# Folding attention's input normalisation into its projection weights, and a new split of the scan input between two engines

## The chip, the core and the metric

The kernel runs on one NeuronCore of one Trainium2 chip. The core has five engines that run their own instruction streams in order and meet at semaphores: PE (TensorE, matrix products), DVE (VectorE, elementwise work and scans), ACT (ScalarE, activations and copies), POOL (GpSimd, elementwise work) and SP (SyncE, which here issues the DMAs). The metric is the time of one execution on the device in microseconds (us); lower is better.

## The reference, cut to what matters

Two layers, each x = x + f(gn(x)), on x of 8 samples x 512 channels x 2304 positions. gn is a group normalisation over 32 groups of 16 channels, without learned scale or shift:

```python
def _gn(v, G=32, eps=1e-5):
    ...
    return ((g - m) / jnp.sqrt(s + eps)).reshape(v.shape)

x = x + _L0_conv_ref(_gn(x), Wq, bq, Wkv, bkv)     # causal linear attention, 8 heads of 64
x = x + _L1_conv_ref(_gn(x), in_proj_w, ...)       # four chained Mamba blocks of 128 channels
```

Attention: q, k, v are W gn(x) + b; Q = elu(q) + 1 and K = elu(k) + 1; the output is the causal sum over positions of (Q_l . K_m) v_m, divided by Q_l . cumsum(K)_l + 1e-10. Mamba: from each block's 128 channels a gate, a short convolution, Silu, and from these the steps delta, B and C; then for 256 channels x 16 states the recurrence h_t = exp(delta_t A) h_(t-1) + delta_t x_t B_t, and y_t = sum over states of h_t C_t. Block s + 1 takes in block s's output.

## The kernel before, in words

**Tiling.** Positions go in six chunks of LC = 384. The Mamba part is 192 *jobs* (8 samples x 4 blocks x 6 chunks); two streams, the even and the odd samples, take turns every six jobs. A job is 8 *slots*; a slot is one half of the 256 channels and 4 of the 16 states, laid out as 128 partitions x 4 groups x 384 positions in a tile u (five buffers). For slot k the program issues

- POOL: `last_product` (L872), the last TAIL = 152 positions of B x (delta x), two slots ahead (L879);
- ACT: `inputs` (L860), a copy of B's first 232 positions for two slots into PSUM (Bp, L863); `decay` (L896), four exponentials of 128x385 into PSUM banks (L900), up to three ahead of the scans (DEPTH);
- DVE: `product` (L887), the first 232 positions (L890), one slot ahead; then four scans (L910);
- POOL: `weigh` (L920), u times C (L923); PE: `gather` (L935), which sums the states by four matmuls into the bank yp (L937), one or two slots later.

`slot` (the loop at the end) writes this order out by hand; every engine runs its list in order. At slot 2 the previous job's sums are gated by DVE (`gated`, L949) and yp is started anew by ACT (`skip`, L868). Slot 7 also issues DVE's product for slot 1 of the next job, behind the one for slot 0 that it issues at its start.

**Tasks beside the slots.** The rest is written as generators that yield due times, counted in half slots; `beside` steps those that are due, twice a slot, so their instructions fall into the engines' lists between scans:

- `statistics` (L225): 24 `bn_stats` on DVE per sample (L253), one every PERIOD = 16 half slots (one job), then `group_norm` (L178), which gives norm[:, 0] = 1/sigma and norm[:, 1] = -mean/sigma per channel (L211). For samples 2 and up it starts so early that two samples' statistics run side by side.
- `chunk` (L280): attention for one sample, 128 output channels o and 384 positions; 192 in all, six to a *part* (sample, o), one per job. In the first part of a sample (o = 0) POOL normalises the input tile xn in four pieces (L324) and it is written to DRAM for the three other parts (L332); PE projects q, k, v (L300, 12 matmuls); ACT takes exp and relu of q and k with the bias (L312, L313); DVE combines them (L359, L367); PE and ACT form the running sum of K (L373, L382), transposes, states and the denominators den (L405); DVE adds 1e-10 and takes the reciprocal (L433, L434); scores, output and state sums follow (L467 to L508). `load_projections` (L99) fetches the next part's weights, two buffers deep, at chunk 4 of 6.
- `prepare` (L710): a job's convolution (L722) and gate matmuls (L733), then on ACT a burst of four Silus (L758 to L763) with an activation table load before and one behind (L900), the steps (L769, L782, L793), delta x on POOL (L834) and the DMAs that spread the rows. The burst falls into slot 7.
- `pass_on` (L578): mixes a block's output into the next block's input and sums the final output on POOL (L696).

The six PSUM banks that decays, projections and all tasks share are handed out in program order (`take`, `Banks`). Before the first job 196 us go into the first statistics and the first chunks of attention; the last dozen jobs have no attention beside them.

Of the kernel before, what the change touches and what calls it, by code (L numbers as in the profile page):

```python
# [9 lines left out]
F32 = mybir.dt.float32  # L10
# [9 lines left out]
LC = 384  # L20
NI, NQ, NGR = 4, 4, 4
SLOTS = 8
TAIL = 152
BANKS = 6
DEPTH = 3
LEAD = 11
# [23 lines left out]
def attention_then_mamba_kernel(  # L50
# [64 lines left out]
    def load_scales():  # L115
# [3 lines left out]
        nc.scalar.activation(w_a, w_a, AF.Exp)  # L119
        nc.scalar.mul(w_a, w_a, -1.0)  # L120

    power = cpool.tile([P, 4], F32, name="power")
    nc.gpsimd.memset(power, -0.5)

# [95 lines left out]

    norms, xns, x1s, done, ksums = {}, {}, {}, {}, {}

    def statistics(b):  # L225

        xv = x[b].rearrange("(t p) l -> p t l", p=P)
        stats = small.tile([P, 4, NC, 6], F32, tag="stats_a", name=f"stats_a{b}", bufs=2)
        if b == 0:

            xs = []

            def load(c):
                t = mpool.tile([P, 4, 1 + LC], F32, tag="u", name=f"xs_{c}", bufs=5)[:, :, 0:LC]
                nc.sync.dma_start(out=t, in_=xv[:, :, c * LC : (c + 1) * LC])
                xs.append(t)

            for c in range(5):
                load(c)
            load_projections()  # L240
            for c in range(NC):
                for ct in range(4):
                    nc.vector.bn_stats(stats[:, ct, c, :], xs[c][:, ct, :])
                if c == 0:
                    load(5)
                    fetch(0)
        else:
            when = begins[b] + b % 2
            for i in range(4 * NC):
                yield (when - 4, 1) if b > 1 else "1", 0  # L250
                xs = piece(b, i)
                yield (when, 1) if b > 1 else "1", 0
                nc.vector.bn_stats(stats[:, i // NC, i % NC, :], xs)  # L253
                when += PERIOD
        norms[b] = yield from group_norm(stats, 4, f"a{b}", 2)

    def piece(b, i):
# [7 lines left out]
    def fetch(m):  # L265

        if m == len(parts):
            return
        b, o, c = parts[m]
        if (o, c) == (0, 0):  # L270
            xns[b] = dpool.tile([512, L], F32, tag="xn", name=f"xn_{b}", bufs=B)
            x1s[b] = dpool.tile([512, L], F32, tag="x1", name=f"x1_{b}", bufs=B)
        xn = apool.tile([P, 4, LC], F32, tag="xn", name=f"xn_{b}_{o}_{c}", bufs=2)
        src = (x[b] if o == 0 else xns[b]).rearrange("(t p) l -> p t l", p=P)
        nc.sync.dma_start(out=xn, in_=src[:, :, c * LC : (c + 1) * LC])
        fetched[m] = xn

    read, passes = [0], {}

    def chunk(m):  # L280

# [9 lines left out]
        def at(j, gap=1):  # L291
            return times[m] + j, gap
# [4 lines left out]
        def project(j):  # L297
            ps = bank()[:, 0:LC]
            for kt in range(4):
                nc.tensor.matmul(  # L300
                    ps,
                    wqs[m // NC][:, kt, j * P : (j + 1) * P],
                    xn[:, kt, :],
                    start=(kt == 0),
                    stop=(kt == 3),
                )
            return ps, bqkv_sb[:, j * 4 + o : j * 4 + o + 1]

        def feature(ps, bias):

# [2 lines left out]
            nc.scalar.activation(ps, ps, AF.Relu, bias=bias)  # L313
            return ex

        if o == 0:
            yield at(-4), 0
            while b not in norms or m not in fetched:
                yield "1w", 0
            xn, norm = fetched.pop(m), norms[b]  # L320
            for ct in range(4):
                if ct:
                    yield at(ct - 4), 0
                nc.gpsimd.tensor_scalar(  # L324
                    xn[:, ct, :],
                    xn[:, ct, :],
                    norm[:, 0, ct : ct + 1],
                    norm[:, 1, ct : ct + 1],
                    ALU.mult,
                    ALU.add,  # L330
                )
# [4 lines left out]
        if o:  # L336
            xn = fetched.pop(m)
# [46 lines left out]
        yield at(7), 0  # L384
        pr = new("pr")
        nc.vector.tensor_mul(pr, q, kc)
        bank.free()
# [2 lines left out]
        for src in (k, vT):  # L390
            ps = bank()[:, 0:LC].rearrange("p (i t) -> p i t", i=NT)
            for i in range(NT):
                nc.tensor.transpose(ps[:, i, :], src[:, subs[i]], ident)
            turned.append(ps)
        yield at(9), 0
        kl, v = new("kl", 1, (P, NT, P)), new("v", 2, (P, NT, P))
        nc.scalar.copy(kl, turned[0])
# [3 lines left out]
        yield at(12), 1  # L401
        both = bank()
        den = both[:, 0 : 2 * NT]
        for i in range(NT):
            nc.tensor.matmul(den[:, 2 * i : 2 * i + 2], pr[:, subs[i]], hsel, start=True, stop=True)  # L405
        more = NT if c + 1 < NC else NT - 1
        ds = both[:, LC - NT * 64 : LC].rearrange("p (i d) -> p i d", i=NT)
        place = range(NT + 1) if c % 2 == 0 else range(NT, -1, -1)
# [113 lines left out]
    class Stream:  # L522
# [55 lines left out]
        def pass_on(self):  # L578
# [78 lines left out]
            for c in range(NC):  # L657
# [13 lines left out]
                if old is None:  # L671
                    nc.scalar.activation(xi[:, icols], xb, AF.Identity, **normed)
                else:
                    bank = Banks()
                    mixed = bank()[:, 0:LC]
                    more = len(factors) == 3
                    for i, src in enumerate((xi[:, icols], fu)):
                        nc.tensor.matmul(  # L678
                            mixed, mix[:, i, :], src, start=i == 0, stop=i == 1, skip_group_check=True
                        )  # L680
                    yield "1", 0
                    nc.scalar.copy(fu, mixed)
# [20 lines left out]
    class Job:  # L703
# [155 lines left out]

        def inputs(self, pair):  # L860

            self.Bp = psx.tile([P, 2, LC - TAIL], F32, tag="Bp", name=f"Bp_{self.n}_{pair}")
            nc.scalar.copy(self.Bp, self.B[pair % 2][:, :, 0 : LC - TAIL])  # L863

        def skip(self, h):

# [4 lines left out]

        def last_product(self, s):  # L872

            shape, cols = [P, NGR, TAIL], slice(LC - TAIL, LC)
            h, q = s // NQ, s % NQ
            u = mpool.tile([P, NGR, 1 + LC], F32, tag="u", name=f"u_{self.n}_{s}", bufs=5)
            if self.c:
                nc.scalar.copy(u[:, :, 0], self.state[:, h, q, :])
            nc.gpsimd.tensor_tensor(  # L879
                u[:, :, 1 + LC - TAIL :],  # L880
                self.B[q // 2][:, q % 2, cols].unsqueeze(1).to_broadcast(shape),
                self.dxr[h][:, :, cols],
                ALU.mult,
# [2 lines left out]

        def product(self, s, u):  # L887

            shape, cols = [P, NGR, LC - TAIL], slice(0, LC - TAIL)
            nc.vector.tensor_mul(  # L890
                u[:, :, 1 : 1 + LC - TAIL],
                self.Bp[:, s % 2, :].unsqueeze(1).to_broadcast(shape),
                self.dxr[s // NQ][:, :, cols],
            )
# [40 lines left out]
        def gather(self, s, u):  # L935
            for g in range(NGR):
# [2 lines left out]
                    state_sum,  # L939
                    u[:, g, 0:LC],  # L940
                    start=False,
                    stop=s % NQ == NQ - 1,
                    skip_group_check=True,
                )

# [211 lines left out]
    def slot(k):  # L1157
# [12 lines left out]
        for i in range(4):  # L1170
# [41 lines left out]
    with tc.manual_schedule():  # L1212
        half_no[0] = FIRST - 6
        Task(statistics(0)).finish()
        load_scales()
        for st in streams:
            tasks.append(Task(st.weights()))
# [94 lines left out]
```

## Time and profile before

| what | value |
|---|---|
| median of 3 runs (range) | 8171.51 us (8164.87 to 8171.61) |
| the profiled execution | 8173.45 us; its span 8171.6 us |
| mean granted TensorE clock in it | 0.945 |
| first scan starts | 196.09 us |
| instructions in the span | 133449 |
| HBM read / written | 1318.23 MB / 327.68 MB |
| DMA engines' mean busy share | 77.8% for the kernel's own queue |

The profile is one execution, seen from the core. A busy share is a mean over the whole span; what bounds a stage is read from the idle time in front of its instructions and from what ended it. In a group line the columns are: line, engine, operation, output <- inputs, shapes, count | busy us, mean ns of one instruction | idle us before it <- what ended that idle time. Instructions on one engine overlap by some 0.05 to 0.1 us, so a stream of 935 ns scans starts one every 0.85 to 0.87 us. Float32 matmuls appear as two records each.

### The profile page before, as it was taken

The numbers are of one execution on the slowest core, as the hardware profiler recorded it, in microseconds if no ns is written. First come the engines' busy times: TensorE is split into PE (matmuls) and PEld (weight loads), VectorE is DVE, ScalarE is ACT, GpSimd is POOL, SyncE is SP. The second block draws the span as 40 slices with busy tenths as digits, with TensorE's granted clock in tenths as the row PEclk, the third lists the DMA queues.
The fourth block names the chain that finished last, engine by engine and source line by source line (L and its number), as shares of the span: only waits on it lengthen the run. The fifth ranks groups of instructions, "written<-read, shape, count | busy, mean of one in ns | idle before, by whom it ended". The sixth has DMA issues, their size and how long they took to land. (4 is left out here: it accounts for less than half of the span.)

```text
span 8171.6 us, 133449 instructions
## 1 busy us (share of the span) xinstructions
PE 7371.7 (90%) x39882; PEld 3532.8 (43%) x39882; DVE 7825.8 (96%) x10534; ACT 6974.3 (85%) x14914; POOL 7747.3 (95%) x3905
## 2 busy tenths in 40 slices
PE   8889999998899999999899999999988999999975
PEld 5444444444444444444444444444444444444421
DVE  3999999999999999999999999999999999999998
ACT  3888888888888888888888888888888888888876
POOL 2999999999999999999999999999999999999999
PEclk9999999999999999999999999999999999999977
DMA  6778888877787788887787788887877777777765
GB/s 199 191 189 207 210 209 212 212 199 210 200 209 204 205 212 212 207 210 201 205 216 205 200 208 209 214 211 195 212 204 204 204 204 200 204 203 199 193 172 148
DMA packets 1097351, 1655.02 MB, mean 203 GB/s; under 512 B 143913, under 2 KB 989353, under 8 KB 1096498
## 3 DMA queue, kind: packets, MB, share of 16 engines
q1 hardware_dynamic: 1096626, 1646.48, 77.8%
q8 instruction: 317, 5.19, 0.3%
q14 instruction: 408, 3.34, 0.1%
HBM read 1318.23 MB, written 327.68 MB: 201 GB/s over the span
## 5 line engine op out<-in xcount | busy, mean ns | idle before, releaser
L910 DVE TENSOR_TENSOR_SCAN u<-bank,u 128x385 f32<-128x385 f32 (+1 forms) x6144 | 5435.3, 935 | 101.6 <-ACT bank L900 101.1
L923 POOL TENSOR_TENSOR u<-u,C 128x1536 f32<-128x1536 f32 x1536 | 4894.4, 3187 | 245.4 <-DVE u L910 164.3
L900 ACT ACTIVATE bank<-dr,scales 128x385 f32<-128x385 f32 (+1 forms) x6144 | 3422.3, 579 | 617.5 <-DVE u L910 573.9
L879 POOL TENSOR_TENSOR u<-B,dxr 128x608 f32<-128x608 f32 x1536 | 2285.6, 1488 | 14.8 <-DMA B<-scr 14.8
L300 PE MATMUL bank<-xn,wq 128*128 128x384 f32 x4608 | 1862.0, 552 | 262.4 <-DVE u L910 215.6
L890 DVE TENSOR_TENSOR u<-Bp,dxr 128x928 f32<-128x928 f32 x1536 | 1682.9, 1096 | 14.9 <-DMA dxr<-xscr 7.7
L937 PE MATMUL yp<-u,cst 128*32 128x384 f32 x12288 | 1357.6, 514 | 259.7 <-POOL u L923 147.7
L300 PEld LDWEIGHTS bank<-xn,wq 128*128 128x128 f32 x4608 | 939.9, 212 | 1153.2 <-DVE u L910 360.5
L722 PE MATMUL bank<-xi,wk 128*128 128x384 f32 x3072 | 1102.4, 502 | 14.5 <-ACT xr L508 13.7
L722 PEld LDWEIGHTS bank<-xi,wk 128*128 128x128 f32 x3072 | 556.2, 191 | 568.2 <-ACT bank L900 77.3
L937 PEld LDWEIGHTS yp<-u,cst 128*32 128x32 f32 x12288 | 249.3, 109 | 904.3 <-issue 412.7
L312 ACT ACTIVATE ex<-bank,bqkv_sb 128x384 f32<-128x384 f32 x384 | 221.1, 576 | 337.0 <-PE bank L300 336.1
L900 ACT ACT_TABLE_LOAD x382 | 490.1, 1283 | 6.9
L863 ACT COPY Bp<-B 128x464 f32<-128x464 f32 x768 | 419.6, 546 | 25.7 <-DMA B<-scr 12.4
L834 POOL TENSOR_TENSOR dx<-delta,xs 128x384 f32<-128x384 f32 x384 | 385.9, 1005 | 21.6 <-ACT delta L793 21.6
L733 PE MATMUL bank<-xi,scales 128*128 128x384 f32 x768 | 325.4, 510 | 50.3 <-ACT xs L758 50.3
L955 PE MATMUL bank<-yz,scales 128*128 128x384 f32 x768 | 328.1, 534 | 37.7 <-DVE yz L949 32.8
L782 PE MATMUL bank<-dbc,steps_w 9*128 9x384 f32 x768 | 306.0, 518 | 21.8 <-DVE rd L433 12.3
L769 PE MATMUL bank<-xs,scales 128*40 128x384 f32 x768 | 285.0, 494 | 0.0
L498 PE MATMUL bank<-sm,v 128*64 128x128 f32 x2304 | 255.2, 300 | 0.0
L793 ACT ACT_TABLE_LOAD x192 | 246.3, 1283 | 3.5
L758 ACT ACT_TABLE_LOAD x192 | 246.3, 1283 | 3.5
(123 smaller groups left out, 8101.2 us busy)
## 6 DMA issues: line engine op xcount, KB each, us to landing
dr<-dscr SPq DMA_DIRECT2D x1536, 192.0 KB, 4.2
dxr<-xscr SPq DMA_DIRECT2D x1536, 192.0 KB, 4.9
xn<-xn SPq DMA_DIRECT2D x192, 768.0 KB, 5.4
B<-scr SPq DMA_DIRECT2D x1536, 96.0 KB, 4.2
C<-scr SPq DMA_DIRECT2D x1536, 96.0 KB, 2.7
dscr<-delta SPq DMA_DIRECT2D x192, 384.0 KB, 5.2
xscr<-dx SPq DMA_DIRECT2D x192, 384.0 KB, 2.9
xn<-in_x SPq DMA_DIRECT2D x48, 768.0 KB, 5.3
```

Source lines behind the costliest of these rows:

```text
L300: nc.tensor.matmul(ps, wqs[m // NC][:, kt, j * P : (j + 1) * P], xn[:, kt, :], start=(kt == 0), stop=(kt == 3),)
L722: nc.tensor.matmul(xc, wk[:, k, h * P : (h + 1) * P], xi[:, c0 + k : c0 + k + LC], start=(k == 0), stop=(k == 3),)
L733: nc.tensor.matmul(zp, w_gate[:, s, h * P : (h + 1) * P], xi[:, c0 + 3 : c0 + 3 + LC], start=True, stop=True,)
L834: nc.gpsimd.tensor_tensor(dx[:, h, :], delta[:, h, :], xs[:, h, :], ALU.mult)
L863: nc.scalar.copy(self.Bp, self.B[pair % 2][:, :, 0 : LC - TAIL])
L879: nc.gpsimd.tensor_tensor(u[:, :, 1 + LC - TAIL :], self.B[q // 2][:, q % 2, cols].unsqueeze(1).to_broadcast(shape), self.dxr[h][:, :, col ...
L890: nc.vector.tensor_mul(u[:, :, 1 : 1 + LC - TAIL], self.Bp[:, s % 2, :].unsqueeze(1).to_broadcast(shape), self.dxr[s // NQ][:, :, cols],)
L900: nc.scalar.activation(dA[:, cols], self.dr[h][:, g, cols], AF.Exp, scale=w_a[:, self.w[1], NGR * h + g, q : q + 1],)
L910: nc.vector.tensor_tensor_scan(u[:, g, cols], dA[:, cols], u[:, g, cols], 0.0, ALU.mult, ALU.add,)
L923: nc.gpsimd.tensor_tensor(u[:, :, 0:LC], u[:, :, 1:], self.C[q // 2][:, q % 2, :].unsqueeze(1).to_broadcast([P, NGR, LC]), ALU.mult,)
L937: nc.tensor.matmul(self.yp[g * 32 : g * 32 + 32, 0:LC], state_sum, u[:, g, 0:LC], start=False, stop=s % NQ == NQ - 1, skip_group_check=True,)
L955: nc.tensor.matmul(self.xm[:, 0:LC], w_out[:, self.w[1], h, :], self.yz[:, h, :], start=(h == 0), stop=(h == 1),)
```

## The change

It has six pieces.

1. **Normalisation in the weights.** POOL's normalisation of xn and its copy in DRAM go; every chunk loads x itself. Instead W (x r + t) + b is computed as (W diag(r)) x + (W t + b): per part, `shifts` sums W t by 12 one-column matmuls, `shifted` adds b by three activations of one column each, and `scaled` multiplies the four 128x384 slices of the weight tile by r on ACT, in place. For the first part this is done by `adapt` ahead of everything; for the others in the last chunk of the part before: the sums are issued behind k's projection, into spare columns of the same bank, their activations behind k's exp and relu, and the scalings one each at four later stages of the chunk.
2. **1e-10 in PSUM.** A matmul of the identity with a constant tile opens den's accumulation; the reciprocal reads den directly, and the addition on DVE goes.
3. **Split of the scan input.** POOL's share is 128 of 384 positions in slots 0 and 1 and 174 in the others, where it was 152 everywhere; DVE's is 256 and 210, where it was 232, and the Bp copies change with it.
4. **State sums.** In slot 0 no sums are issued; in slot 1 those of the last two slots of the job before are, the later slot's first.
5. **Statistics** of samples 4 to 7 begin 23 or 24 jobs earlier and come every second job, even and odd samples in turn.
6. **The output sum** on POOL waits until 17 half slots before the job that the chunk is for, slot 7 of an earlier job; it was issued some six half slots before that.

```diff
-TAIL = 152
+WIDE, TAIL = 128, 174
...
+    def shifts(i, to):
+        w, norm = wqs[i], norms[parts[i * NC][0]]
+        for j in range(3):
+            for kt in range(4):
+                nc.tensor.matmul(
+                    to[:, j : j + 1],
+                    w[:, kt, j * P : (j + 1) * P],
+                    norm[:, 1, kt : kt + 1],
+                    start=(kt == 0),
+                    stop=(kt == 3),
+                    skip_group_check=True,
+                )
+
+    def shifted(i, shift):
+        o = parts[i * NC][1]
+        biases[i] = bias = small.tile([P, 3], F32, tag="bias", name=f"bias_{i}", bufs=2)
+        for j in range(3):
+            nc.scalar.activation(
+                bias[:, j : j + 1],
+                shift[:, j : j + 1],
+                AF.Identity,
+                bias=bqkv_sb[:, j * 4 + o : j * 4 + o + 1],
+            )
+
+    def scaled(i, kt):
+        w, norm = wqs[i], norms[parts[i * NC][0]]
+        nc.scalar.activation(w[:, kt, :], w[:, kt, :], AF.Copy, scale=norm[:, 0, kt : kt + 1])
...
-        if o == 0:
...
-                nc.gpsimd.tensor_scalar(
...
-            save(xns[b].rearrange("(t p) l -> p t l", p=P)[:, :, cols], xn)
...
         kp, kb = project(1)
+        ahead_of = m // NC + 1 if c == NC - 1 and m + 1 < len(parts) else None
+        if ahead_of is not None:
+            extra = bank.held[-1][:, LC : LC + 3]
+            shifts(ahead_of, extra)
         yield at(3), 0
         ex = feature(kp, kb)
+        if ahead_of is not None:
+            shifted(ahead_of, extra)
         yield at(4), 0
...
+        if ahead_of is not None:
+            scaled(ahead_of, 0)
         yield at(6), 0
+        if ahead_of is not None:
+            scaled(ahead_of, 1)
...
+        nc.tensor.matmul(den, ident, tiny, start=True, stop=False, skip_group_check=True)
...
-        nc.vector.tensor_scalar_add(rd, den, 1e-10)
-        nc.vector.reciprocal(rd, rd)
+        nc.vector.reciprocal(rd, den)
...
+                    yield (first - 17, 1) if not last else "1", 0
                     nc.gpsimd.tensor_tensor(xa, xa, fu, ALU.add)
...
-            shape, cols = [P, NGR, TAIL], slice(LC - TAIL, LC)
+            tail = TAIL if s > 1 else WIDE
+            shape, cols = [P, NGR, tail], slice(LC - tail, LC)
...
+        if b > 3:
+            begins[b] -= (4 * NC - b % 2) * PERIOD
...
-                if len(waiting) > 1:
+                if s == 1:
+                    for i in range(len(waiting) - 2, -1, -1):
+                        waiting.pop(i)()
+                elif s and len(waiting) > 1:
                     waiting.pop(0)()
```

More of the change, by code (lines that the diff above doesn't have):

```diff
@@ L120, in load_scales @@
         nc.scalar.mul(w_a, w_a, -1.0)
+    tiny = cpool.tile([P, 2 * LC // T], F32, name="tiny")
+    nc.gpsimd.memset(tiny, 1e-10)
     power = cpool.tile([P, 4], F32, name="power")
@@ L219, in group_norm @@
         return norm
-    norms, xns, x1s, done, ksums = {}, {}, {}, {}, {}
+    norms, x1s, done, ksums = {}, {}, {}, {}
     def statistics(b):
@@ L247, in statistics @@
         else:
-            when = begins[b] + b % 2
+            when, gap = begins[b] + (b % 2 if b < 4 else 0), PERIOD if b < 4 else 2 * PERIOD
             for i in range(4 * NC):
@@ L253, in statistics @@
                 nc.vector.bn_stats(stats[:, i // NC, i % NC, :], xs)
-                when += PERIOD
+                when += gap
         norms[b] = yield from group_norm(stats, 4, f"a{b}", 2)
@@ L270, in fetch, with adapt @@
         if (o, c) == (0, 0):
-            xns[b] = dpool.tile([512, L], F32, tag="xn", name=f"xn_{b}", bufs=B)
             x1s[b] = dpool.tile([512, L], F32, tag="x1", name=f"x1_{b}", bufs=B)
         xn = apool.tile([P, 4, LC], F32, tag="xn", name=f"xn_{b}_{o}_{c}", bufs=2)
-        src = (x[b] if o == 0 else xns[b]).rearrange("(t p) l -> p t l", p=P)
+        src = x[b].rearrange("(t p) l -> p t l", p=P)
         nc.sync.dma_start(out=xn, in_=src[:, :, c * LC : (c + 1) * LC])
         fetched[m] = xn
-    read, passes = [0], {}
+    read, passes, biases = [0], {}, {}
+    def shifts(i, to):
[23 more added lines that the diff above has]
+        nc.scalar.activation(w[:, kt, :], w[:, kt, :], AF.Copy, scale=norm[:, 0, kt : kt + 1])
+    def adapt():
+        bank = Banks()
+        yield FIRST - 6, 1
+        while 0 not in norms:
+            yield "1w", 1
+        shift = bank()
+        shifts(0, shift)
+        shifted(0, shift)
+        bank.free()
+        for kt in range(4):
+            scaled(0, kt)
     def chunk(m):
@@ L306, in project @@
                 )
-            return ps, bqkv_sb[:, j * 4 + o : j * 4 + o + 1]
+            return ps, biases[m // NC][:, j : j + 1]
         def feature(ps, bias):
@@ L314, in feature @@
             return ex
-        if o == 0:
[L317 to L323, printed above, removed]
-                nc.gpsimd.tensor_scalar(
[L325 to L331, printed above, removed]
-            save(xns[b].rearrange("(t p) l -> p t l", p=P)[:, :, cols], xn)
+        while m not in fetched:
+            yield "1w", 0
         while read[0] < m - 1:
@@ L335, in chunk @@
         yield at(0), 1
-        if o:
-            xn = fetched.pop(m)
+        xn = fetched.pop(m)
+        assert m // NC in biases
         if c == 0:
@@ L384, in chunk @@
         yield at(7), 0
+        if ahead_of is not None:
+            scaled(ahead_of, 2)
         pr = new("pr")
@@ L394, in chunk @@
             turned.append(ps)
+        yield at(8), 0
+        if ahead_of is not None:
+            scaled(ahead_of, 3)
         yield at(9), 0
@@ L403, in chunk @@
         den = both[:, 0 : 2 * NT]
+        nc.tensor.matmul(den, ident, tiny, start=True, stop=False, skip_group_check=True)
         for i in range(NT):
-            nc.tensor.matmul(den[:, 2 * i : 2 * i + 2], pr[:, subs[i]], hsel, start=True, stop=True)
+            nc.tensor.matmul(
+                den[:, 2 * i : 2 * i + 2],
+                pr[:, subs[i]],
+                hsel,
+                start=False,
+                stop=True,
+                skip_group_check=True,
+            )
         more = NT if c + 1 < NC else NT - 1
@@ L860, in inputs @@
         def inputs(self, pair):
-            self.Bp = psx.tile([P, 2, LC - TAIL], F32, tag="Bp", name=f"Bp_{self.n}_{pair}")
-            nc.scalar.copy(self.Bp, self.B[pair % 2][:, :, 0 : LC - TAIL])
+            width = LC - (TAIL if pair else WIDE)
+            Bp = psx.tile([P, 512], F32, tag="Bp", name=f"Bp_{self.n}_{pair}")
+            self.Bp = Bp[:, 0 : 2 * width].rearrange("p (f l) -> p f l", f=2)
+            nc.scalar.copy(self.Bp, self.B[pair % 2][:, :, 0:width])
         def skip(self, h):
@@ L879, in last_product @@
             nc.gpsimd.tensor_tensor(
-                u[:, :, 1 + LC - TAIL :],
+                u[:, :, 1 + LC - tail :],
                 self.B[q // 2][:, q % 2, cols].unsqueeze(1).to_broadcast(shape),
@@ L887, in product @@
         def product(self, s, u):
-            shape, cols = [P, NGR, LC - TAIL], slice(0, LC - TAIL)
+            width = LC - (TAIL if s > 1 else WIDE)
+            shape, cols = [P, NGR, width], slice(0, width)
             nc.vector.tensor_mul(
-                u[:, :, 1 : 1 + LC - TAIL],
+                u[:, :, 1 : 1 + width],
                 self.Bp[:, s % 2, :].unsqueeze(1).to_broadcast(shape),
@@ L941, in gather @@
                     start=False,
-                    stop=s % NQ == NQ - 1,
+                    stop=s % NQ == (NQ - 1 if s < NQ else NQ - 2),
                     skip_group_check=True,
@@ L1214, in attention_then_mamba_kernel @@
         Task(statistics(0)).finish()
+        Task(adapt()).finish()
         load_scales()
```

## The prediction, made before the changed kernel had run

> **What bounds the kernel now.** I read the page first: busy times, then the costliest groups.
>
> ```profile
> PE 7371.7 (90%) x39882; PEld 3532.8 (43%) x39882; DVE 7825.8 (96%) x10534; ACT 6974.3 (85%) x14914; POOL 7747.3 (95%) x3905
> ...
> L910 DVE TENSOR_TENSOR_SCAN u<-bank,u 128x385 f32<-128x385 f32 (+1 forms) x6144 | 5435.3, 935 | 101.6 <-ACT bank L900 101.1
> L923 POOL TENSOR_TENSOR u<-u,C 128x1536 f32<-128x1536 f32 x1536 | 4894.4, 3187 | 245.4 <-DVE u L910 164.3
> ...
> L879 POOL TENSOR_TENSOR u<-B,dxr 128x608 f32<-128x608 f32 x1536 | 2285.6, 1488 | 14.8 <-DMA B<-scr 14.8
> ...
> L890 DVE TENSOR_TENSOR u<-Bp,dxr 128x928 f32<-128x928 f32 x1536 | 1682.9, 1096 | 14.9 <-DMA dxr<-xscr 7.7
> ```
>
> DVE and POOL are both nearly full. DVE's waits are few and short; the largest is for ACT's decays. So I cut the trace into jobs (32 scans each) and took the windows view of four: two plain jobs, then two of a stretch in which POOL also normalises (L324). Columns: window, then busy time of PE, PEld, DVE, ACT, POOL.
>
> ```profile
> 2487.80:2528.20 40.40, 37.94 (x210) 18.34 (x209) 39.50 (x52) 36.54 (x81) 39.49 (x19) 0.96 0.82 218
> 2773.10:2813.50 40.40, 37.05 (x216) 17.95 (x217) 39.96 (x54) 36.49 (x81) 39.50 (x19) 1.00 0.79 204
> 1890.40:1933.20 42.80, 38.70 (x233) 18.61 (x233) 41.09 (x57) 36.51 (x74) 42.80 (x24) 0.96 0.82 210
> 2023.10:2067.60 44.50, 39.30 (x215) 18.62 (x216) 39.82 (x53) 36.66 (x81) 43.71 (x25) 0.92 0.79 203
> ```
>
> A plain job takes 40.40 us whether DVE does 54 things or 52: the extra input statistics fill a hole in slot 7, where ACT loads the Silu table, does four activations and reloads the exp table while DVE runs out of decays (0.87 us in the first, 0.41 in the second). Everywhere else DVE is the path, and POOL has 0.9 us to spare. In the normalising stretches POOL is full and jobs take 43.
>
> **The change, part by part** (against the profiled execution: 8173.45 us, span 8171.6; the median shown is 8171.51, 2 us less).
>
> *1. Widths.* DVE's product goes from 928 elements to 1024 for slots 0 and 1 and to 840 for slots 2 to 7. The same operation on 384 elements (L386) takes 541 ns, so an element costs (1096 - 541)/544 = 1.02 ns: +0.10 us twice, -0.09 six times. Both wide products are issued in slot 7, inside the hole, so there they cost nothing; if the hole is filled by two statistics per job (some 20 jobs of samples 2 and 3; later samples are spread to one per job) they cost 0.20. Gain 0.54 us a job, 0.34 in those 20.
>
> POOL takes 6 x 88 - 2 x 96 = 336 more elements a job. From its own two rows an element is (3187 - 1488)/928 = 1.83 ns, or 0.62 us a job; the upper end is the whole 1488/608 = 2.45 ns, 0.82 us. In the 35 jobs from 2324.9 to 3762.1 (41.06 us each, POOL busy 1388.86, 39.68 each) that makes 40.30 for POOL, against 41.06 - 0.71 = 40.35 for DVE after parts 1 and 2: level. In a plain job POOL is the longer by 0.4, but its share of u lies ready a slot ahead of the scan, so it can trail and catch up where DVE has extra work or waits (part 4 gives it such waits). The Trainium skill ("GPSIMD Engine Reference", section 3.1) gives 2.6 cycles an element for two inputs at 1.2 GHz, 2.17 ns: an estimated 0.73 us, by which POOL would be the bound and the sum some 9 us worse; the two rows say less for the increment. The move of the output sum (L696) from slot 5 to slot 7 takes 1.0 us from where POOL runs behind to where it waits for a scan; I count it as nothing.
>
> *2. One DVE instruction less per chunk.* L433 (141 ns; the reciprocal starts 0.17 us after it) goes: -0.17 us a job. The extra matmul that adds 1e-10 is one of three like L405 and hides behind the state sums.
>
> Ordinary jobs: 180 jobs hold attention work, 30 of them are priced in 4. 130 x 0.54 + 20 x 0.34 + 150 x 0.17 = 103 us. PE's run from slot 2 to slot 7 has 0.5 us of slack (below) and POOL none, so I take 0.9 of it: **-93** (ends -50 and -105).
>
> *3. Normalisation off POOL.* The three stretches of 13 jobs take 559.4, 554.1 and 559.2 us; 35 plain-stretch jobs take 1437.2, 41.06 each. Excess: 1672.7 - 39 x 41.06 = 71 us. Some stays: the statistics' own chain (one square of four columns takes 4.56 us at 1935.4, a wait for POOL's power 2.2 us) and an odd long wait, about 8 us a stretch. **-45** (ends -25 and -65). 128 us of POOL time (192 x 0.67) goes, but 119 us comes back by part 1.
>
> *4. Weights and bias sums, once per part.* The last chunk of a part now issues 12 one-column matmuls behind k's projection, three small activations, and four scalings of a 128x384 weight tile on ACT. Neither hides. PE in such a job (the second plain one above holds a last chunk), from k's projection on:
>
> ```profile
> 2785.85 2.85 PE L300 MATMUL bank<-xn,wq 128*128 128x384 f32 x8
> 2788.54 0.49 PE L457 MATMUL bank<-bar,ident_b 128*128 128x384 bf16 x2
> ...
> 2805.75 2.85 PE L722 MATMUL bank<-xi,wk 128*128 128x384 f32 x8
> 2808.44 1.69 PE L733 MATMUL bank<-xi,scales 128*128 128x384 f32 x4
> ```
>
> and ACT at the two ends of that run:
>
> ```profile
> 2788.74 0.58 ACT L312 ACTIVATE ex<-bank,bqkv_sb 128x384 f32<-128x384 f32 x1 [1.12 <-PE bank L300]
> 2789.22 0.55 ACT L313 ACTIVATE bank<-bank,bqkv_sb 128x384 f32<-128x384 f32 x1
> 2789.68 1.21 ACT L900 ACTIVATE bank<-dr,scales 128x385 f32<-128x385 f32 x2
> ...
> 2809.06 0.57 ACT L761 ACTIVATE xs<-bank,scales 128x384 f32<-128x384 f32 x1
> ```
>
> PE is busy 27.44 of the 28.1 us from 2784.5 to 2812.6. The nearest row for a sum is L405: two columns move through 128x128 weights, six records (three matmuls) in 0.83 us. Twelve are 24 records: 3.3 us. The Trainium skill ("TensorE: Matmul & The Clock Gate", section on LDWEIGHTS) speaks against the change here: a weight load takes columns/1.2 ns however little moves, so 24 loads are an estimated 2.6 us, and the sum would fall by 0.7 us a job; the trace's rate is the slower.
>
> The built program shows more: ACT's exp for k waits for a PE count that is raised once, behind the twelfth sum, and the bias activations have no PE wait of their own. So k's features wait out the sums, too. Exp, relu and three bias activations stand ahead of the two decays at 2789.68 in ACT's queue, and k's product on DVE (2790.18, 0.4 us after relu ended) stands ahead of two scans. DVE loses 3.3 - 0.1 (exp had just become free) - 0.4, some 2.7 us, there. ACT's four scalings, 0.5 to 0.6 us each (a plain copy of that size, L441, is 495 ns), roughly fill the 2.2 us that ACT waits for DVE in slots 4 to 7. PE's delay runs on, with no gap to swallow it, to the second convolution, which ends at 2808.6 and is wanted at 2809.06: 0.5 us of slack. The Silu burst is so 2.8 us late and DVE's hole as much later than today; the stall at k and the one at the burst are the same delay seen twice, plus up to 0.6 where ACT's extra work tells. **3.1 us** a job, net of what such a job gains by parts 1 and 2 before the burst. Ends: 0 if all hid, 5.5 if the two stalls added. 30 jobs: **+93** (ends 0 and +165).
>
> *5. Ends.* Start: the first chunk waits for the sums and scalings instead of POOL's pieces (+2; PE's first 24 projections already take 11.07 us instead of 8.55), one more set of sums while PE is full (+3), the added matmuls (+2): **+7** (0 to 12). Tail: the last dozen jobs have no attention work and POOL is full in eight (472.31 of 483.8 us busy): 8 x 0.62 = **+5** (0 to 8).
>
> Sum: -93 - 45 + 93 + 7 + 5 = -33; 8173 - 33 = **8140 us**, 0.4% less.
>
> **The rivals.**
> - *The sums hide.* For: ACT is idle 3.9 us a job. Against: PE is not, and the shared wait. Then part 4 is nothing, its 30 jobs gain like the others, and POOL, without waits to catch up in, sets the end: at most 41.06 - 40.30 = 0.76 a job, DVE allows 0.7, say 0.65: -117 - 45 + 12 = -150: 8025.
> - *The sums stall DVE twice (slower).* The place is the last chunk of each part: DVE waits 2.7 us at k's product, and again in slot 7, because ACT's scalings ahead of the burst do not fit into its waits. At 5.5 to 6.2 us a job that is +165 to +186: -33 - 93 + 186 = +60: 8230. It decides from 4.7 us a job. For: ACT is in order and the burst is its last piece before the hole. Against: ACT's waits in slots 4 to 7 are about as long as the scalings.
> - *Ordinary jobs do not get shorter.* PE's run is 23.5 us of back-to-back work with 0.5 us to spare; if PE, not DVE, sets slots 2 to 7, part 1 brings half: +47: 8187, no measurable change.
>
> **How the numbers follow.** About 0.2% (16 us) is what a measurement of this kernel can tell from no change. Forecast 0.50 (its own range 8100 to 8170), sums hidden 0.12, ordinary jobs unchanged 0.20, two stalls 0.18. Faster than 8155: 0.43 of the forecast's 0.50, the 0.12, and 0.05 of the third: 0.60. Slower than 8188: the 0.18 and a little of the third: 0.20. The rest, 0.20, is no change. The range 8055 to 8195 leaves out most of the first rival and half of the second.
>
> **What would show it.** Right: plain jobs of 39.7 to 40.1 us with POOL full; every sixth job 43 to 44 us, with DVE idle before k's product and in slot 7, PE full between; no wait of PE for the input tile; jobs of the three stretches like the others. Wrong: sums much shorter than 3.3 us, ordinary jobs at 40.4, or DVE waiting for POOL's product, which no row does now.

## The result, and the profile after

The changed kernel takes **8197.08 us** (median of 8 runs, 8189.03 to 8216.24), the kernel before 8171.56 (8 runs, 8162.23 to 8178.92) beside it: ratio 1.0036, 95% interval 1.0026 to 1.0046. It is 0.36% slower; the forecast was 0.4% faster. The profiled execution took 8191.43 us, span 8189.7. The mean granted TensorE clock is 0.925 in it, 0.945 before.

The page of the changed kernel, busy times and the groups that answer to those of before (L963 the scans, L976 GpSimd's product with C, L931 and L943 the two halves of the scan input):

```profile
PE 7587.3 (93%) x41034; PEld 3707.6 (45%) x41034; DVE 7800.9 (95%) x10342; ACT 7030.1 (86%) x15138; POOL 7763.9 (95%) x3714
...
L963 DVE TENSOR_TENSOR_SCAN u<-bank,u 128x385 f32<-128x385 f32 (+1 forms) x6144 | 5440.4, 936 | 82.4 <-ACT bank L953 81.5
L976 POOL TENSOR_TENSOR u<-u,C 128x1536 f32<-128x1536 f32 x1536 | 4902.7, 3192 | 209.3 <-DVE u L963 170.8
...
L931 POOL TENSOR_TENSOR u<-B,dxr 128x696 f32<-128x696 f32 (+1 forms) x1536 | 2433.9, 1585 | 15.6 <-DMA dxr<-xscr 11.5
```

POOL's product (L931, 2433.9 us) rose by 148 us; its normalisation had taken 128. DVE's busy time hardly fell, by 25 us, although its product (L943, 1619.0 us against 1682.9) and the dropped additions (27.2) make 91. Something on DVE grew by 66. The windows view of four neighbouring jobs, the third with a last chunk (columns as before; the last three are the granted clock, the DMA share and GB/s), shows where:

```profile
2694.08:2738.28 44.20, 40.51 (x215) 18.91 (x213) 43.95 (x57) 35.73 (x75) 40.84 (x20) 0.92 0.73 191
2738.28:2778.25 39.97, 38.24 (x215) 18.97 (x213) 39.63 (x52) 36.40 (x81) 39.74 (x19) 0.96 0.81 221
2778.25:2822.58 44.33, 43.88 (x239) 22.66 (x237) 40.02 (x52) 38.74 (x88) 40.89 (x20) 0.88 0.71 191
2822.58:2863.04 40.46, 39.78 (x217) 19.36 (x217) 40.37 (x57) 36.86 (x82) 40.23 (x20) 0.92 0.76 199
```

The second and fourth are ordinary jobs, 39.97 and 40.46 us (39.7 to 40.1 were forecast, 40.40 was the plain job before). The third has the forecast stall: 44.33 us, of which DVE is idle 4.3, 3.0 of them ahead of k's product. The first was not in the forecast: 44.20 us, and DVE *busy* 43.95. It is the job in which a block hands over to the next (`pass_on`). The groups view of DVE has one line there that nobody would look at, an addition of 1 to two numbers per partition:

```profile
L641 DVE TENSOR_SCALAR wt<-wt 128x2 f32<-128x2 f32 x32 | 85.9, 2684 | 0.3 <-ACT wt L639 0.3
```

In the kernel before the same line is L593:

```profile
L593 DVE TENSOR_SCALAR wt<-wt 128x2 f32<-128x2 f32 x32 | 29.7, 929 | 0.3 <-ACT wt L591 0.3
```

There most of the 32 instructions take 0.24 to 0.41 us. The timeline around one of them, changed kernel (columns: start, us, engine, line, operation, tiles):

```profile
2709.83 3.22 POOL L976 TENSOR_TENSOR u<-u,C 128x1536 f32<-128x1536 f32 x1
...
2711.34 4.30 DVE L641 TENSOR_SCALAR wt<-wt 128x2 f32<-128x2 f32 x1
...
2712.97 1.04 POOL L883 TENSOR_TENSOR dx<-delta,xs 128x384 f32<-128x384 f32 x1
2713.92 1.70 POOL L931 TENSOR_TENSOR u<-B,dxr 128x696 f32<-128x696 f32 x1
...
2715.68 0.17 DVE L642 RECIPROCAL wt<-wt 128x2 f32<-128x2 f32 x1
2715.76 1.78 DVE L963 TENSOR_TENSOR_SCAN u<-bank,u 128x384 f32<-128x384 f32 x2
```

and in the same job of the kernel before:

```profile
2706.53 3.19 POOL L923 TENSOR_TENSOR u<-u,C 128x1536 f32<-128x1536 f32 x1
...
2709.36 0.38 DVE L593 TENSOR_SCALAR wt<-wt 128x2 f32<-128x2 f32 x1
...
2709.66 1.01 POOL L834 TENSOR_TENSOR dx<-delta,xs 128x384 f32<-128x384 f32 x1
```

The addition ends 20 to 30 ns after a GpSimd instruction ends, in both kernels and every time but the last, when GpSimd has nothing left to do. Before, it met the last 0.36 us of L923. Now GpSimd runs 1.35 us later against DVE: the addition meets a weighing with 1.7 us to go, and when that ends, GpSimd's next two instructions go first as well. Of the 27 that take over 1 us (5 before), 11 wait out one instruction (1.4 us) and 16 those queued behind it, too (3.7 us and more). What decides between the two is not shown. It is not a gap on GpSimd: its next instruction is recorded as starting where the one before ends in all 27, and in the kernel before as well (L834 above). DVE runs in order, so the next scans wait. The profile books all of it as busy time.

**Theory T1**: the addition needs something that GpSimd holds while it works; the new split makes GpSimd trail, so that the addition meets more of GpSimd's work. **Rivals**: T2, it waits for its operand (ACT's exp, L639); T3, it comes from the new order (the output sum, the state sums), not from the split.

### The profile page after: what moved, and what is told of

It reads as the page before. It is cut to its first block, busy times and chain, and to the rows that moved or that the text cites. A ratio compares the mean times of both kernels' runs of the same rounds, so it can differ in the third digit from the quotient of the medians.

```text
span 8189.7 us, 135414 instructions
## 1 busy us (share of the span) xinstructions
PE 7587.3 (93%) x41034; PEld 3707.6 (45%) x41034; DVE 7800.9 (95%) x10342; ACT 7030.1 (86%) x15138; POOL 7763.9 (95%) x3714
## 5 line engine op out<-in xcount | busy, mean ns | idle before, releaser
L963 DVE TENSOR_TENSOR_SCAN u<-bank,u 128x385 f32<-128x385 f32 (+1 forms) x6144 | 5440.4, 936 | 82.4 <-ACT bank L953 81.5
L976 POOL TENSOR_TENSOR u<-u,C 128x1536 f32<-128x1536 f32 x1536 | 4902.7, 3192 | 209.3 <-DVE u L963 170.8
L931 POOL TENSOR_TENSOR u<-B,dxr 128x696 f32<-128x696 f32 (+1 forms) x1536 | 2433.9, 1585 | 15.6 <-DMA dxr<-xscr 11.5
L990 PE MATMUL yp<-u,cst 128*32 128x384 f32 x12288 | 1514.8, 583 | 298.1 <-POOL u L976 189.9
L341 PE MATMUL bank<-xn,wq 128*128 128x384 f32 x4608 | 1766.3, 530 | 9.8 <-DVE u L963 6.6
L943 DVE TENSOR_TENSOR u<-Bp,dxr 128x840 f32<-128x840 f32 (+1 forms) x1536 | 1619.0, 1054 | 16.8 <-DMA dxr<-xscr 15.9
L990 PEld LDWEIGHTS yp<-u,cst 128*32 128x32 f32 x12288 | 298.3, 119 | 1110.2 <-issue 649.6
L353 ACT ACTIVATE ex<-bank,bias 128x384 f32<-128x384 f32 x384 | 221.2, 576 | 365.2 <-PE bank L341 246.5
L831 PE MATMUL bank<-dbc,steps_w 9*128 9x384 f32 x768 | 365.4, 602 | 87.3 <-DVE rd L482 35.1
L914 ACT COPY Bp<-B 128x420 f32<-128x420 f32 (+1 forms) x768 | 406.3, 529 | 37.9 <-DMA B<-scr 33.2
L1008 PE MATMUL bank<-yz,scales 128*128 128x384 f32 x768 | 291.1, 500 | 8.2 <-DVE yz L1002 6.4
L930 ACT COPY u<-state 128x4 f32<-128x4 f32 x1280 | 249.8, 195 | 5.3 <-PE yp L990 4.0
```

The lines of the kernel that those rows point to most:

```text
L341: nc.tensor.matmul(ps, wqs[m // NC][:, kt, j * P : (j + 1) * P], xn[:, kt, :], start=(kt == 0), stop=(kt == 3),)
L831: nc.tensor.matmul(vp, steps_w[32:41, s, h * P : (h + 1) * P], dbc[32:41, :], start=True, stop=True)
L914: nc.scalar.copy(self.Bp, self.B[pair % 2][:, :, 0:width])
L931: nc.gpsimd.tensor_tensor(u[:, :, 1 + LC - tail :], self.B[q // 2][:, q % 2, cols].unsqueeze(1).to_broadcast(shape), self.dxr[h][:, :, col ...
L943: nc.vector.tensor_mul(u[:, :, 1 : 1 + width], self.Bp[:, s % 2, :].unsqueeze(1).to_broadcast(shape), self.dxr[s // NQ][:, :, cols],)
L963: nc.vector.tensor_tensor_scan(u[:, g, cols], dA[:, cols], u[:, g, cols], 0.0, ALU.mult, ALU.add,)
```

## The experiments

All times are medians; the ratio is to the kernel before on the same chip, with its 95% interval. e3 and e6 leave the normalisation of the later parts out of the computation; they price the work and are no versions to use.

| run | us | ratio |
|---|---|---|
| e1: changed kernel, addition as two one-column ones | 8122.90 | 0.9942 (0.9929 to 0.9954) |
| e2: kernel before, the same | 8151.19 | 0.9978 (0.9968 to 0.9987) |
| e3: changed, no sums and scalings for later parts | 8104.51 | 0.9916 (0.9902 to 0.9929) |
| e4: changed, even split | 8172.21 | 1.0000 (0.9991 to 1.0008) |
| e5: e1 with even split | 8151.35 | 0.9978 (0.9969 to 0.9987) |
| e6: e1 with e3's edit | 8009.88 | 0.9803 (0.9789 to 0.9816) |
| e7: e1, k's features ahead of the sums | 8197.65 | 1.0033 (1.0021 to 1.0046) |
| e8: e1, sums spread, in the bank of den | 8293.18 | 1.0148 (1.0134 to 1.0161) |
| e9: as e8, bank of their own | 8352.22 | 1.0223 (1.0209 to 1.0237) |
| e10: as e7, bank of their own | 8382.03 | 1.0258 (1.0244 to 1.0273) |
| e11: e1, one-column operations in the statistics' chain | 8101.38 | 0.9916 (0.9902 to 0.9929) |
| e12: e11, sums spread, at their old place | 8103.49 | 0.9918 (0.9905 to 0.9932) |
| e13: changed, addition reads PSUM | 8236.62 | 1.0080 (1.0066 to 1.0094) |
| e14: e11, share of 166 for 174 | 8102.46 | 0.9915 (0.9901 to 0.9929) |

### Splitting the addition (e1, e2)

```diff
-                nc.vector.tensor_scalar_add(wt[:, 0:2], wt[:, 0:2], 1.0)
+                nc.vector.tensor_scalar_add(wt[:, 0:1], wt[:, 0:1], 1.0)
+                nc.vector.tensor_scalar_add(wt[:, 1:2], wt[:, 1:2], 1.0)
```

> The changed kernel with one edit: the addition of 1 to two columns (L641, DVE, once per block, 32 times, 85.9 us in all, mean 2684 ns; 29.7 us and 929 ns in the kernel before at L593) is written as two additions of one column each. Theory T1, that this instruction with a two-column operand waits for GpSimd to finish, and that one-column DVE instructions of the same kind do not (L194, 273 ns): the two additions take 0.3 us each, some 50 to 65 us of the 85.9 go, and the kernel takes 8130 to 8150 us. Rival T2, that it waits for its operand, ACT's exp at L639, whose end the profile models too early: the first of the two additions takes as long as before and the time stays at 8190 to 8200. Rival T2b, that the wait goes but GpSimd is the bound and hands the gain back: additions short, time above 8180.

> The kernel before with the same split of its addition at L593 (29.7 us in 32 instructions). T1: a gain of 10 to 20 us, 8150 to 8162, since only about a third of its 32 waited. T2: no change, 8171. With the run of the changed kernel it also gives the change without this wait on both sides: T1 expects the ratio of the two split kernels to be below 1.

e1 gained 74 us, more than the 8130 to 8150 expected, and e2 18.7. The groups of e1:

```profile
L641 DVE TENSOR_SCALAR wt<-wt 128x1 f32<-128x1 f32 x32 | 4.6, 145 | 0.3 <-ACT wt L639 0.3
L642 DVE TENSOR_SCALAR wt<-wt 128x1 f32<-128x1 f32 x32 | 4.5, 142 | 0.0
```

85.9 us became 9.1; none of the 64 is over 0.16 us, although 62 of them run inside a GpSimd instruction and GpSimd is as busy as in the changed kernel (7757.4 us against 7763.9). The operand comes from the same exp, so T2 is out. Hand-over jobs (the 29 with attention beside them) fall from a median of 43.91 us to 40.10. The granted clock is the same in the runs of both (0.924 to 0.927), so the 74 us do not hang on it. With the addition split on both sides the change is a gain: 8122.90 against 8151.19, 28 us.

### The split back to even (e4, e5)

```diff
-WIDE, TAIL = 128, 174
+WIDE, TAIL = 152, 152
```

> The changed kernel with the split of the scan input back at 152 columns in every slot; all other pieces of the change stay. GpSimd's row falls by 336 elements a job, 0.7 us. If GpSimd, which trails, is what made the two-column addition long (T1 in its full form): L641 is back to a mean of 0.9 to 1.2 us (30 to 40 us in all) and jobs that open an attention part's statistics lose their long square and add at L200 and L201; DVE pays 0.36 to 0.54 us a job, 60 to 95 us, so 8200 to 8240 in all. If the wait came with the moved output sum or the swapped state sums and not with the split: L641 stays at 2.7 us, and the time goes to 8260 to 8290. If GpSimd has been the bound of ordinary jobs, so that wider shares brought nothing: time below 8170.

> The changed kernel with the two one-column additions and the split of the scan input back at 152 columns everywhere: against the run with the two additions alone (8122.9) it shows what the new split is worth when no DVE instruction waits for GpSimd. By my term for the widths, DVE pays 0.36 (the wide products hidden: 8 x 1096 against 2 x 1198 + 6 x 1006 is 0.34) to 0.54 us a job over 150 to 180 jobs: 8177 to 8220. If GpSimd, whose increment is 0.77 us a job, takes back most of what DVE gains: 8135 to 8160. The even split left 34.6 us in L641, of which 25 go.

The line in e4:

```profile
L641 DVE TENSOR_SCALAR wt<-wt 128x2 f32<-128x2 f32 x32 | 34.6, 1080 | 0.3 <-ACT wt L639 0.3
```

Over 1 us in 6 of 32 (5 before the change): the split makes it long, and T3 is out. In time e4 missed every expectation; it gained 25 us where I had it lose. e5, inside its second range, says how much the split brings: without the long addition 28 us (8151.35 to 8122.90), not the 54 and more that I had from DVE's rows. With the addition in place it costs 25. So the same edit changes sign with one small instruction, a swing of 53 us.

### What the sums cost (e3, e6, e12)

```diff
-            return ps, biases[m // NC][:, j : j + 1]
+            bias = biases[0][:, j : j + 1] if m < NC else bqkv_sb[:, j * 4 + o : j * 4 + o + 1]
+            return ps, bias
...
-        ahead_of = m // NC + 1 if c == NC - 1 and m + 1 < len(parts) else None
+        ahead_of = None
```

> The changed kernel without the bias sums, their activations and the weight scalings of all parts but the first (31 of 32): later parts use the raw weights and biases, so their normalisation is left out of the computation. It prices the work in the last chunk of each part (my +93 us, 3.1 us a job). If the stall at k's features is a real loss of DVE time: 70 to 95 us less than the changed kernel, 8100 to 8125, and last-chunk jobs as short as their neighbours. Rival, that GpSimd takes the place of the stall as the bound (its row for 696 elements is 1683 ns, 0.77 us a job more than before): under 40 us, 8155 or more.

> The two one-column additions, and the bias sums, their activations and the scalings of all parts but the first left out (later parts use raw weights and biases, as before in such a run). With the additions split, a last-chunk job takes a median of 44.13 us against 39.97 for the job ahead of it, 4.1 more than an ordinary job and not 3.1: part of the stall had been overlaid by the long addition two slots of work earlier in the chain. If that is so, leaving the sums out is worth 30 x 3.7 to 4.1, 110 to 125 us: 8000 to 8015. If GpSimd sets the end once DVE is not stalled: no more than the 93 us that it was worth in the changed kernel, 8030 or above.

e3 is 93 us faster than the changed kernel, e6 113 faster than e1. In e6 a last-chunk job is as short as its neighbours (39.98). The difference of e1's and e6's 30 last-chunk jobs is 115.5 us, 3.85 each; by the idle times in the two traces 100.0 of it are DVE's wait ahead of k's product. Between the changed kernel and e3 it is 3.35 each, 100 us; e3 gained less than that in all: its addition is longer still (103.5 us), and its hand-over jobs outside the three stretches take 12 us more. So the rival, GpSimd as the bound, was wrong.

e12 spreads a part's sums from one job to three, four each, at the same place (with weights and statistics earlier):

```diff
-        if ahead_of is not None:
+        js = [c - 3] if m > NC and c > 2 else []
...
+        if js:
             extra = bank.held[-1][:, LC : LC + 3]
-            shifts(ahead_of, extra)
+            shifts(following, extra, js)
```

> The run with one-column operations in the statistics' chain (8101.4), with the 12 sums of a part (from the third on) spread over its predecessor's last three chunks, four each, at the same place as in the changed kernel: behind k's projection, in its bank, with one bias activation each. No bank changes hands for them, so no new wait comes in. If the price of the sums has a threshold (ACT and TensorE have about 0.5 us to spare at this place in a job, the four sums take 0.9), a part costs 3 x 0.4 to 0.9 us instead of 4.1: 8030 to 8075. If the price goes by the us of sums alone, it stays: 8095 to 8110. If each interruption costs more than its sums: above 8110.

```profile
DVE k L411 <- ACT bias L307: 106.4, 91, 5.3
```

In this waits view of e12 (total us, times, longest) the wait at k is three times as frequent as in e11 and sums to about the same (97.2 us, 31 times there); outside the three stretches the jobs of the three phases take a median of 40.98, 40.89 and 41.08 us where e11 has 40.10, 39.98 and 44.13. The price goes roughly by the length of the sums; four of them do not stay below a threshold.

### Moving the sums (e7, e8, e9, e10)

e7 issues the sums behind k's features, in the same bank; e8 issues four in each of three chunks behind the state sums, where PE waits for GpSimd; e9 and e10 repeat e8 and e7 with a fresh bank. The heart of e8 and of e9:

```diff
         nc.scalar.copy(S[:, kept_states, :], ds[:, 0:more, :])
+        if part is not None:
+            shifts(part, both[:, LC : LC + 3], [c - 2])
```

```diff
+            yield at(14), 1
+            other = Banks()
+            extra = other()[:, 0:3]
+            shifts(part, extra, [c - 2])
```

> The two one-column additions, and in the last chunk of a part k's exp and relu are put ahead of the 12 sums in program order, so that they wait for k's projection alone; the bias activations come behind k's product, before the bank is freed. The sums stay on TensorE at the same place. My step in the prediction, that the stall at k's product and the one at the Silu burst are one delay seen twice: DVE's wait at k (105 us, 31 times) goes, and comes back as waits for decays or at later attention steps, 8105 to 8130. Rival, that the wait at k was the loss and TensorE's 2.7 us are taken up by gaps behind it: 8020 to 8060.

> The two one-column additions, and the 12 sums of a part (from the third part on) spread over three chunks: four each behind the state sums of chunks 2, 3 and 4 of the part before, where TensorE waits for GpSimd's product (slot 0), with one bias activation each; the scalings stay in the last chunk. Weights are fetched three chunks earlier and a sample's statistics end 48 half slots earlier. If the sums hide in TensorE's idle time of slots 0 and 1 (some 1.8 us of 12.3, 0.9 us wanted): within 40 us of the run without the sums, 8010 to 8055. If TensorE's run has no room anywhere, each set costs its 0.9 us: 85 us come back, 8090 to 8120.

> As the run with the sums spread over chunks 2, 3 and 4, but into a PSUM bank of their own. In that run TensorE stood still 90 times, 1.87 us each (169.0 us), ahead of the sums (L285) for ACT's copy of S out of the same bank (L488), although they write other columns of it; that wait, and not the sums' own time, is my explanation of 8293.2. If so, the wait goes, and the sums cost what they move: between 8010 (hidden) and 8100 (0.9 us each in three of six jobs, 85 us above the 8009.9 without sums). If the time stays above 8200, TensorE has no room in slot 0 and the explanation is wrong.

> As the run with k's features ahead of the sums, but the 12 sums go into a bank of their own, so that k's product, which waited 103.3 us for L285 in that run (31 times), no longer has a reason to. My step that the stall at k and the one in slot 7 are one delay seen twice: the wait at k goes, the delay is found later in the job, and the last-chunk jobs stay at 42.5 to 44 us: 8085 to 8125. Rival, that only the wait at k cost time: last-chunk jobs at 40 to 41.5, 8015 to 8055. Slower than 8130 if the extra bank delays decays.

All four lost, and none came into a range in which the sums get cheaper. In e7 the wait at k only changed its name, since product and sums share a bank (DVE's waits); the last-chunk jobs are 2.2 us longer yet than in e1 (a median of 46.28 us against 44.12), and waits for decays grew from 79.3 to 114.4 us:

```profile
DVE k L397 <- PE bank L285: 103.3, 31, 6.5
```

In e8 and e9 PE itself stands before the sums (L285; PE's waits, e8 first):

```profile
PE bank L285 <- ACT S L488: 169.0, 90, 2.7
```

```profile
PE bank L285 <- ACT delta L855: 307.7, 90, 3.7
```

In this program a write into spare columns of a bank waits for those who still read the rest of it, and a fresh bank is one whose last reader, here ACT's delta, is still behind. e9 was to free e8 of its wait and nearly doubled it. So it does not test the explanation of e8, which I had called wrong beforehand if e9 came out above 8200: that e8's wait (169.0 us) is about as long as its loss against e1 (170 us) fits the explanation and does not show it. In e10, outside the three stretches, the last-chunk job took a median of 44.91 us and the job behind it 48.94 (e1: 40.43). DVE's wait for the bias at k is gone, and its waits for decays are 174.5 us (e1: 79.3), as the third branch of the expectation has it, but I have not isolated which bank began it. Whether the stall at k would move to slot 7 therefore stays open.

### What in the instruction waits (e11, e13), and GpSimd's share (e14)

```diff
-            nc.vector.tensor_mul(gm[:, 2, :], gm[:, 1, :], gm[:, 1, :])
-            nc.vector.tensor_add(gm[:, 2, :], gm[:, 2, :], mv[:, :, 1])
+            for ct in range(n):
+                nc.vector.tensor_scalar(
+                    gm[:, 2, ct : ct + 1],
+                    gm[:, 1, ct : ct + 1],
+                    gm[:, 1, ct : ct + 1],
+                    mv[:, ct, 1:2],
+                    ALU.mult,
+                    ALU.add,
+                )
```

> The two one-column additions, and in the input statistics' chain the square and the addition over four columns (L200, L201: two operands in SBUF, 3.17 and 1.58 us where they met a GpSimd instruction, 26.8 us in 16 instructions) become four one-column operations that square and add in one. If what makes a DVE instruction wait is a second operand or a second column in SBUF: these take 0.15 us each, 15 to 22 us less than 8122.9, 8100 to 8110. If the time of these chains is hidden (DVE has room there): within 5 us of 8122.9.

```diff
-                nc.scalar.activation(wt[:, 0:2], wt[:, 2:4], AF.Exp, scale=-1.0 / L)
+                nc.scalar.activation(ew, wt[:, 2:4], AF.Exp, scale=-1.0 / L)
...
-                nc.vector.tensor_scalar_add(wt[:, 0:2], wt[:, 0:2], 1.0)
+                nc.vector.tensor_scalar_add(wt[:, 0:2], ew, 1.0)
```

> The changed kernel with the two-column addition kept as one instruction, but with ACT's exp written to two columns of a PSUM bank, so that the addition reads PSUM and writes SBUF. If the wait is for SBUF access that GpSimd holds and a one-operand instruction takes only when its operand and its result both lie in SBUF: L641's successor takes under 0.3 us and the time is that of the split additions, 8120 to 8135 (a few us more if the lent bank delays a decay). If it is the number of columns: it stays at 2.7 us on average, 8185 to 8205.

```diff
-WIDE, TAIL = 128, 174
+WIDE, TAIL = 128, 166
```

> The run with one-column operations in the statistics' chain (8101.4), with GpSimd's share in slots 2 to 7 at 166 columns instead of 174: 192 elements a job less for GpSimd (0.41 us at 2.14 ns), 192 more for DVE (0.20 us at 1.02 ns). If DVE sets the ordinary jobs: 150 to 180 x 0.20, 25 to 35 us more, 8127 to 8137. If GpSimd does: less than 8090. If both are level, within 10 us of 8101.

The groups of e11 and of e13:

```profile
L201 DVE TENSOR_SCALAR gm_a<-gm_a,mv_a 128x1 f32<-128x1 f32 x32 | 6.5, 267 | 0.3
```

```profile
L643 DVE TENSOR_SCALAR wt<-bank 128x2 f32<-128x2 f32 x32 | 4.8, 151 | 0.2 <-ACT bank L641 0.2
```

e11 took 26.8 us of DVE time to 6.5 and gained 21.5 us. In e13 two columns read from PSUM do not wait, so it is not their number alone: source and result both lie in SBUF where the addition waits. The kernel as a whole was yet slower than the changed one, against the expectation: hand-over jobs took 43.89 us, and the wait for K's running sum (DVE pr, from ACT's L418) grew from 33.8 us in e1 to 101.6. The lent bank, and the half slot at which it is taken, are the other differences; no run shows by what path they cost time. e14 is level with e11: neither GpSimd nor DVE alone sets ordinary jobs there.

The Trainium skill ("SBUF — State Buffer", section on who interferes with whom) says that VectorE and GpSimd share a pair of SBUF ports: VectorE contends for it when it reads two SBUF tensors and when it runs in a two-port mode, and in that mode whoever issues first has the pair for the whole instruction. "VectorE: DVE Perf Modes" (section on what auto-detection checks) gives the two-port mode 2x to an instruction whose single source and destination are in SBUF, with outermost non-unit dimensions both even or equal. The runs agree: additions of two columns within SBUF wait (over 1 us in 27 of 32), of one column (0 of 64) and of two from PSUM (0 of 32) do not. L200, with two SBUF operands and four columns, waits too (3.17 us in the median); no run separates its second operand from its width. The runs show blocking, not the ports themselves.

**The version that beats both kernels is e11**: 8101.38 us, 0.84% below the kernel before (e12 and e14 are level with it).

## Why the prediction was wrong

The forecast was 8140; the time is 57 us above it, and the long addition grew by 56. The step that failed is that POOL's share lies ready a slot ahead, **"so it can trail and catch up"**, a trailing that the sum put at nothing. Trailing was free for those who wait on POOL's *results* (the changed kernel, too, has no DVE wait for its product); it was not for L641, which uses none: its 32 instructions went from 29.7 to 85.9 us, and without the wait in them the kernel takes 74 us less (e1). I had looked for the first kind alone ("DVE waiting for POOL's product"). The hint was in what I wrote, the square of four columns with 4.56 us, which I filed under the statistics' own chain.

The terms that the sum did have are best checked with the addition split on both sides (e2 to e1, job by job in the profiled executions): their sum was -33 and measures -27.

- **1 and 2, ordinary jobs, -93 by 150 jobs of 0.62 us: the size came out, by luck.** 120 plain jobs without a last chunk lost 70.3 us, 0.59 each. Inside it two errors cancel. DVE's rows came as forecast (1198 ns for 1024 elements, 1006 for 840), but the split itself brings 0.28 us a job (e5 to e1, 33.7 us over the same 120) and not 0.54; the other pieces bring 0.30 together (e2 to e5), not 0.17, and no run tells them apart.

```profile
L931 POOL TENSOR_TENSOR u<-B,dxr 128x696 f32<-128x696 f32 x1152 | 1939.1, 1683 | 1.3 <-DMA B<-scr 1.2 <-POOL u L976 0.2
L931 POOL TENSOR_TENSOR u<-B,dxr 128x512 f32<-128x512 f32 x384 | 494.8, 1289 | 14.3 <-DMA dxr<-xscr 11.5 <-DMA fu<-fm 2.7
...
L943 DVE TENSOR_TENSOR u<-Bp,dxr 128x840 f32<-128x840 f32 x1152 | 1159.0, 1006 | 0.4
...
L943 DVE TENSOR_TENSOR u<-Bp,dxr 128x1024 f32<-128x1024 f32 x384 | 460.0, 1198 | 16.4 <-DMA dxr<-xscr 15.9 <-issue 0.3 <-DMA B<-scr 0.2
```

- **POOL's element price was too low.** By these rows of the changed kernel 696 elements take 1683 ns, 512 take 1289: 2.14 ns, not 1.83, 0.72 us a job for 336 elements. The estimate of 2.17 ns from the Trainium skill ("GPSIMD Engine Reference", section 3.1) lies near that; the slope between two different lines (L923 and L879) was a poor guide. By e14 it did not make POOL the bound.
- **3, normalisation off POOL, -45: right.** The 30 jobs of the three stretches that hold no last chunk lose 61.5 us, of which 30 x 0.59 is term 1: 44 remain.
- **4, the sums, +93: right in place, somewhat large.** The 30 jobs cost 82.3 us net, 2.74 each and not 3.1. The timeline of the changed kernel in the third job above:

```profile
2793.88 2.73 PE L285 MATMUL bank<-norm_a,wq 128*128 128x1 f32 x24
...
2796.65 0.58 ACT L353 ACTIVATE ex<-bank,bias 128x384 f32<-128x384 f32 x1 [3.74 <-PE bank L285]
2797.13 0.55 ACT L354 ACTIVATE bank<-bank,bias 128x384 f32<-128x384 f32 x1
2797.71 0.56 ACT L298 ACTIVATE bias<-bank,bqkv_sb 128x1 f32<-128x1 f32 x3
...
2798.31 0.55 DVE L399 SCALAR_TENSOR_TENSOR k<-ex,bank 128x384 f32<-128x384 f32 x1 [3.03 <-ACT bias L298]
```

  24 records take 2.73 us, nearer to the 2.6 estimated from the Trainium skill ("TensorE: Matmul & The Clock Gate", section on LDWEIGHTS) than to my 3.3. The exp waits behind the twelfth sum, and k's product behind the bias activations. DVE's largest wait ahead of k's product, the changed kernel first, then the kernel before:

```profile
DVE k L399 <- ACT bias L298: 98.1, 31, 5.3
```

```profile
DVE k L367 <- ACT bank L313: 14.2, 9, 3.7
```

  No second stall of like size follows: in the 30 jobs DVE's waits ahead of scans sum to 12.2 us (15.5 in the kernel before). So the slower rival had the right sign by the wrong mechanism.
- **5, start +7, tail +5: too small.** From e2 to e1 the first scan comes 14 us later (10 from the kernel before to the changed one, 206.08 us), the last dozen jobs take 5.7 us more, and 2.4 us more lie behind the last scan.

The third rival, "ordinary jobs do not get shorter", lies near in time (8187) and is refuted by the jobs, which lost 0.59 us each. Its premise that the split brings half is what was measured (0.28 of 0.54); that PE is the reason, as it says, no run tests, and e14 shows only that neither GpSimd nor DVE alone is the bound.

## What to carry to other kernels

When an engine is filled up, ask not only who waits for its results but which instructions of other engines cannot run while it runs; here 32 additions of two numbers per partition cost 56 us more once GpSimd ran some 1.35 us later beside them. Such a wait hides in *busy* time: look at groups whose mean is far above what their size explains, or whose mean and median part (in the kernel before: 929 and 380 ns), before trusting a busy share. Moving work into an idle engine's gap is not free if it needs a buffer: the readers of that buffer become its wait (e8, e9).

## What the runs showed of the hardware

- A DVE instruction that waits for GpSimd need not get the next turn: in 16 of 27 cases GpSimd instructions queued behind the running one went first, and an addition that takes 0.17 us beside an idle GpSimd took 3.7 to 7.0 us. In the other 11 it went first (1.4 us).
- A reciprocal of two columns, SBUF to SBUF, did not wait, where an addition of the same shape does: in e1 27 of 32 ran wholly inside a GpSimd instruction, and none of the 32 took over 0.17 us (one at 2696.90, inside a GpSimd instruction from 2694.92 to 2698.16).
